# Two freed LSTM state tiles take x of groups 4 to 11, value staging gets a second tile, and scratch writes are queued behind the value moves

## The chip, the cores and the metric

The kernel runs on one core of a Trainium2 chip. The metric is the device time of one execution in microseconds (us); of three runs of the kernel before, the median is 2487.06 us (2484.32 to 2489.86). A profiled execution of its own took 2489.89 us; the span that the profile covers is 2488.1 us of it.

Engines are named as in the profile: PE (TensorE, matmuls), DVE (VectorE), ACT (ScalarE), POOL (GpSimd) and SP (SyncE, which here only issues DMAs). PEld is the loading of a matmul's stationary operand.

## The reference: four layers on x of 128 x 64 x 256

`x` holds 128 batches of 64 nodes with 256 features. Each layer normalizes x over the features, applies relu, and adds the layer's output to x:

```python
h = jnp.maximum(_layernorm(x, axis=-1), 0.0)
x = x + _L0_gnn_ref(h, adj, ...)     # two graph convolutions, then LSTMs over windows of 1 to 4 nodes
h = jnp.maximum(_layernorm(x, axis=-1), 0.0)
x = x + _L1_gnn_ref(h, W, adj)       # attention with 4 heads of 64, masked by adj
...                                  # layer 2: graph convolution and two linears with batch norm
...                                  # layer 3: three graph convolutions
```

The change touches the seam between layer 0 and layer 1. In layer 0, for p = 1 to 4 in turn, an LSTM is run over each window of p nodes, and its last hidden state replaces the features of the window's last node:

```python
for p in range(1, MAX_SKIP + 1):
    nw = Tv // p
    wins = h[:, :nw * p, :].reshape(Bv * nw, p, Hd)
    last = _lstm_last(Wih[p - 1], Whh[p - 1], bih[p - 1], bhh[p - 1], wins)
    idx = jnp.arange(nw) * p + (p - 1)
    h = h.at[:, idx, :].set(last.reshape(Bv, nw, Hd))
```

Layer 1 computes q, k and v from h with one weight matrix, a masked softmax of q k / 8 over the 64 nodes of a batch, and its product with v.

## The kernel before, in words

**Tiling.** The 8192 tokens (batch and node) are 16 groups `g` of 512 tokens, 8 batches each. A group of x is a tile of 128 x 4 x 256 numbers, 512 KB. Layer 0 holds its state with features on partitions, in four tiles `hs[0]` to `hs[3]` (`h0` to `h3`) of 32 batches each, so one of them belongs to four groups of x. They stand in a pool of their own on the right side of the on-chip memory.

**End of layer 0.** The LSTMs with p = 4 run in two passes: `j = 0` works on `h0` and `h1`, `j = 2` on `h2` and `h3`. So `h0` and `h1` are final before the second pass begins. Step t of a pass is done for two units in turn (`i` = 0 and 1) by `next_step`: two gate sets of seven products each (a Strassen-like scheme, `seven`, with its combining sums on ACT, DVE and POOL). During steps t = 1 and 2 of pass `j = 2`, four slots of code turn `h0` and `h1` back to token order: `turn_nodes(j, turned)` transposes 16 nodes by two DVE instructions (L262) into a staging tile and writes it with four DMAs on SP's queue (L265) to a scratch tensor `ys` in HBM. `add_turned(g)` (L271) then adds the scratch to `xs[g]` with an accumulating DMA that POOL issues. At this point only groups 0 to 3 of x are on the chip, and only these are added here.

**Layer 1, the attention loop.** It runs over the 16 groups. Group g does: the first half of the values (`values(hT_all, v, (0,))`: 4 matmuls L873, an ACT copy `vt` L878, 4 DMAs L881 on SP's queue that move the halves of `vt` to the partitions of `v`), the load of x of group g + 5 (L58, SP's queue), the seven products of q and k (L851, combined on ACT, DVE and POOL; the POOL part is L180), the addition of the output of group g - 2 (L959 on DVE, L962 on POOL), the turning of the softmax of group g - 1 (L934, copied by ACT L937), the second half of the values, the accumulating DMA `add_turned(g + 3)` for g = 1 to 12, the transposes of the next group's h (L127, copied by ACT L282, differences on DVE L286, L290, L291), the product of softmax and values of group g - 1 (`attend`, L947), the scores of group g (L898, masked by DVE L905), its softmax (L916, L917, ACT L918), one `turn_nodes(g + 8)` for g < 8 (this turns `h2` and `h3`), and the normalization of group g + 2 (DVE L832 to L837, POOL L836 and L838, ACT L111).

`vt` has one buffer. The tile that `turn_nodes` fills in the loop has one buffer too (tag `hc`). Tiles for x of groups 4 to 15 come from a pool `xres_b` that is opened after the LSTM's pools are closed.

**What sets the order.** Each engine works through its instructions in one order, fixed when the kernel is built; a planner of the tile framework merges the program's pieces by its own estimate of when each can start, with `issue_after(x)` as a lower bound ("not ahead of x"). So a change of buffers or of the program's order can move instructions of other lines as well. Waits are semaphore waits that the framework derives from the tiles.

Of the kernel before, what the change touches and what calls it, by code (L numbers as in the profile page):

```python
# [8 lines left out]
F32 = mybir.dt.float32  # L9
# [5 lines left out]
P = 128  # L15
D = 256
NODES = 64
# [21 lines left out]
def adj_preln_kernel(ctx: ExitStack, tc: tile.TileContext, x_in, adj, vec, bg0, bg1,  # L39
# [17 lines left out]
    def load_x(x, g):  # L57
        nc.sync.dma_start(out=x, in_=x_view[:, g * GT : (g + 1) * GT, :])  # L58
# [181 lines left out]


    with tc.using_default_side("right"):
        hres_pool = tc.tile_pool(name="hres", bufs=1)
        hres = hres_pool.__enter__()
    hs = [
        hres.tile([P, 2, NODES, HB], F32, tag=f"h{i}", name=f"h{i}")
        for i in range(NTOK // (HB * NODES))
    ]

    turned_pool = ctx.enter_context(  # L250
        tc.tile_pool(name="turned", bufs=1, space=bass.MemoryType.DRAM)
# [42 lines left out]
    with tc.tile_pool(name="lw", bufs=5) as lw:  # L294
# [220 lines left out]
        with tc.tile_pool(name="back", bufs=1, reuse_waits="tile") as back_pool, \  # L515
# [196 lines left out]
            for p, nk in ((1, 8), (2, 8), (3, 7), (4, 8)):  # L712
# [7 lines left out]
                for j in range(0, len(units), 2):  # L720
# [23 lines left out]
                    for t in range(1, p):  # L744
                        for i, u in enumerate(two):
                            next_step(t, p, n, u, ws, last_sum if (j, t, i) == (0, 1, 0) else None)

                            if p == 4 and j == 2 and t < p - 1:
                                slot = 2 * t + i - 2
                                if slot == 0:  # L750
                                    room = keep.tile([P, 2, TN, 2, 32], F32, tag="arena", name="turned")
                                for part in range(2 * slot, 2 * slot + 2):
                                    turn_nodes(
                                        part,
                                        room[:, part % 3] if part % 3 < 2 else back_pool.tile(
                                            [P, TN, 2, 32], F32, tag="hc", name="turned"
                                        ),
                                    )
                                if slot > 1:
                                    for x_of_group in range(2 * slot - 4, 2 * slot - 2):  # L760
                                        add_turned(x_of_group)
                            if p == 4 and j == 2 and t == p - 1 and i == 0:

                                h = back_pool.tile([P, GT, D], F32, tag="hc", name="h")
                                ln_relu(xs[0], h)
                                hTs = keep.tile([P, 2, 2, GN], F32, tag="arena", name="hT")
                                hT = features(transposed(h))

    xpool_b = ctx.enter_context(tc.tile_pool(name="xres_b", bufs=1, reuse_waits="tile"))
    for g in range(NK, NG):  # L770
        xs.append(xpool_b.tile([P, GT, D], F32, tag=f"x{g}", name=f"x{g}"))
        if g == NK:
            load_x(xs[g], g)


    def arena(pool):
# [42 lines left out]
        return counted  # L819


    with tc.tile_pool(name="att", bufs=2, reuse_waits="tile") as ap_:
        shifts_made = []

# [40 lines left out]
        def values(hT, v, ks):  # L865


            for k in ks:
                ps = bank((P, 2, D))
                for t in range(2):  # L870
                    tok = (2 * k + t) * P
                    for c in range(2):
# [5 lines left out]
                nc.scalar.copy(vt, ps)  # L878
                for par in range(2):
                    for b in range(2):  # L880
# [92 lines left out]
        last = None  # L973
        for g in range(NG):
            if g == NG - NK + 1:
                hres_pool.__exit__(None, None, None)
                with tc.using_default_side("right"):
                    ar_right = ctx.enter_context(
                        tc.tile_pool(name="arena_r", bufs=NG // 2, reuse_waits="tile")
                    )  # L980
            hT_all, blocks = hT
            v = ap_.tile([P, 2 * GT, P], F32, tag="v", name="v")
            moved = values(hT_all, v, (0,))
            if g + NK + 1 < NG:
                with tc.issue_after(moved):
                    load_x(xs[g + NK + 1], g + NK + 1)
            q, k, finish = queries_keys(blocks)
            if g == 0:
                h = normalized(1)
# [10 lines left out]
            if g == NG - 1:  # L1000
# [590 lines left out]
```

## Time and profile before

| what | value |
|---|---|
| median of 3 runs | 2487.06 us (2484.32 to 2489.86) |
| the profiled execution | 2489.89 us, its span 2488.1 us |
| PE busy | 2455.0 us (99%) |
| DVE, ACT, POOL busy | 1539.1 us (62%), 1126.0 us (45%), 454.7 us (18%) |
| attention loop, first L873 of group 0 to first L873 of group 15 | 1207.88 to 1450.49 us |
| x loads on SP's queue | 27 of 512 KB, median 4.8 us from issue to landing |
| scratch writes on SP's queue | 64 of 128 KB, median 3.5 us |
| accumulating loads of POOL | 16 of 512 KB, median 7.3 us |
| value moves on SP's queue | 128 of 64 KB, median 2.1 us |

Times in the profile are counted from the span's start. A timeline or group line names the engine, the source line and "out<-in" by the program's tile names; what stands in brackets after it is how long the engine had been idle and what released it. Lines of a table over stretches of time give, for each engine, the time that it was busy and in parentheses the number of its instructions. A PE that waits inside a long queue of matmuls can look busy, because the ends of matmuls are modelled.

### The profile page before, as it was taken

How to read it: one execution, taken by the hardware profiler on the slowest of the kernel's cores; microseconds unless marked ns; L12 is line 12 of the kernel's file. 1: busy time of each engine (PE TensorE's matmuls, PEld its weight loads, DVE VectorE, ACT ScalarE, POOL GpSimd, SP SyncE). 2: the span in 40 equal slices, each digit the busy share in tenths (PEclk: the TensorE clock that was granted, in tenths of full speed). 3: DMA queues.
4: the chain of work that ended last, by engine and by line, in shares of the span. 5: the costliest groups of instructions: out<-in, count | busy, mean ns of one | idle time of the engine just before them, and what ended most of it. 6: DMA issues, size and time to landing. Idle time of an engine off the chain costs nothing.

```text
span 2488.1 us, 46519 instructions
## 1 busy us (share of the span) xinstructions
PE 2455.0 (99%) x19628; PEld 2091.2 (84%) x19628; DVE 1539.1 (62%) x2768; ACT 1126.0 (45%) x2026; POOL 454.7 (18%) x392
## 2 busy tenths in 40 slices
PE   9999999999999999999989899999999999999999
PEld 6678888889999988888878764486998898888888
DVE  6668866666566575675687686576556454454544
ACT  4557745444444443443544466564333333333332
POOL 4432211111111111121133331013111111101110
PEclk9999999999999999999999999999999999999999
DMA  3200000000000000160265410010000000000000
GB/s 131 88 2 1 1 17 1 1 1 34 1 1 1 1 1 1 24 92 1 63 117 119 91 40 2 1 48 13 10 9 19 10 10 10 18 10 10 18 10 18
DMA packets 123568, 64.79 MB, mean 26 GB/s; under 512 B 70496, under 2 KB 119776, under 8 KB 123360
## 3 DMA queue, kind: packets, MB, share of 16 engines
q1 hardware_dynamic: 113920, 52.62, 8.2%
q0 software_dynamic: 8448, 8.39, 2.3%
q8 instruction: 154, 2.52, 0.4%
q10 hardware_dynamic: 992, 0.82, 0.1%
q14 instruction: 54, 0.44, 0.1%
HBM read 36.64 MB, written 16.78 MB: 21 GB/s over the span
## 4 chain that ended last, share of the span: by engine, by line
PE 87%; DVE 5%; ACT 2%; DMA 2%; issue 1%; POOL 1%; SPq 1%; DVEq 0%; POOLq 0%; ACTq 0%
PE ps L548 39%; PE ps L1391 16%; PE ps L1436 8%; PE ps L804 4%; PE ps L144 4%; PE ps L1355 3%; PE ps L491 2%; PE ps L851 2%; PE ps L467 2%; PE ps L1173 2%; PE ps L1224 2%; DMA v<-vt 1%; PE ps L873 1%; ACT arena L229 1%; POOL arena L180 1%
## 5 line engine op out<-in xcount | busy, mean ns | idle before, releaser
L548 PE MATMUL ps<-diff,s 128*128 128x256 f32 (+1 forms) x1824 | 393.5, 371 | 0.9 <-DVE diff L668 0.9
L1391 PE MATMUL ps<-arena 128*128 128x256 f32 x1792 | 392.4, 381 | 0.0
L1391 PEld LDWEIGHTS ps<-arena 128*128 128x128 f32 x1792 | 337.9, 190 | 54.0 <-issue 9.3
L548 PEld LDWEIGHTS ps<-diff,s 128*128 128x128 f32 x1824 | 345.9, 190 | 33.8 <-issue 1.6
L562 ACT ACTIVATE gates<-gates,lbias 128x512 f32<-128x512 f32 (+5 forms) x426 | 244.2, 620 | 206.0 <-DVE gates L185 149.3
L180 POOL TENSOR_TENSOR gates<-p 128x512 f32<-128x512 f32 (+1 forms) x115 | 149.2, 1297 | 885.7 <-DVE p L177 834.9
L548 PE MATMUL ps<-h,w 128*128 128x256 f32 (+1 forms) x1028 | 241.0, 371 | 0.0
L548 PE MATMUL ps<-diff,w 128*128 128x256 f32 (+1 forms) x1040 | 238.8, 371 | 1.1 <-DVE p L177 1.1
L548 PEld LDWEIGHTS ps<-diff,w 128*128 128x128 f32 x1040 | 197.3, 190 | 19.7 <-DVE p L177 1.5
L548 PEld LDWEIGHTS ps<-h,w 128*128 128x128 f32 x1028 | 195.0, 190 | 19.2 <-issue 0.5
L562 ACT ACTIVATE gates<-ps,lbias 128x256 f32<-128x256 f32 (+3 forms) x213 | 91.8, 477 | 242.5 <-PE ps L548 242.4
L180 POOL TENSOR_TENSOR arena<-arena 128x256 f32<-128x256 f32 (+1 forms) x73 | 82.0, 1123 | 587.8 <-DVE arena L177 558.1
L229 ACT ACTIVATE arena<-arena 128x512 f32<-128x512 f32 (+1 forms) x160 | 88.7, 582 | 193.4 <-POOL arena L180 101.6
L1436 PE MATMUL ps<-arena 128*128 128x128 f32 x1280 | 149.7, 276 | 0.0
L185 DVE TENSOR_TENSOR gates<-p,ps 128x512 f32<-128x512 f32 (+1 forms) x115 | 76.3, 664 | 113.9 <-PE ps L548 113.7
L1436 PEld LDWEIGHTS ps<-arena 128*128 128x128 f32 x1280 | 145.5, 192 | 1.1
L185 DVE TENSOR_TENSOR arena<-arena,ps 128x256 f32<-128x256 f32 (+1 forms) x73 | 43.5, 597 | 156.7 <-PE ps L1391 87.0
L176 DVE TENSOR_TENSOR p<-p,ps 128x512 f32<-128x512 f32 (+1 forms) x131 | 87.0, 664 | 64.6 <-PE ps L548 46.4
L548 PE MATMUL ps<-state,w 128*128 128x256 f32 (+1 forms) x512 | 116.1, 370 | 0.9 <-ACT p L173 0.8
L189 DVE TENSOR_TENSOR gates<-p,ps 128x512 f32<-128x512 f32 (+1 forms) x115 | 76.6, 666 | 64.2 <-PE ps L548 63.7
L804 PE MATMUL ps<-arena,w 128*128 128x512 f32 x256 | 116.0, 606 | 0.0
L548 PE MATMUL ps<-state,s 128*128 128x256 f32 (+1 forms) x512 | 115.8, 369 | 0.0
(196 smaller groups left out, 4062.6 us busy)
## 6 DMA issues: line engine op xcount, KB each, us to landing
x<-in_x SPq DMA_DIRECT2D x27, 512.0 KB, 4.8
y<-turned SPq DMA_DIRECT2D x64, 128.0 KB, 3.5
x<-y POOLq DMA_DIRECT2D x16, 512.0 KB, 7.3
v<-vt SPq DMA_DIRECT2D x128, 64.0 KB, 2.1
out<-x SPq DMA_DIRECT2D x15, 512.0 KB, 2.9
w<-in_wih SPq DMA_DIRECT2D x4, 1024.0 KB, 7.4
w<-in_whh SPq DMA_DIRECT2D x3, 1024.0 KB, 4.9
arena<-in_l3w SPq DMA_DIRECT2D x3, 1024.0 KB, 5.0
```

The lines of the kernel that those rows point to most:

```text
L144: last = nc.tensor.matmul(pss[b][half * 64 : half * 64 + 64, c, t, :], lhsT=src[rows, t, col : col + 64], rhs=a2[rows, :], start=True, sto ...
L176: nc.vector.tensor_tensor(p1, p1, ps[2], ALU.add)
L180: nc.gpsimd.tensor_tensor(out=out[1][1], in0=p1, in1=p5, op=ALU.add)
L185: nc.vector.tensor_tensor(out[0][1], p1, ps[1], ALU.add)
L189: last = nc.vector.tensor_tensor(to, p, q, ALU.add)
L229: nc.scalar.activation(o, o, func)
L548: nc.tensor.matmul(ps[:, r], lhsT=wc[:, j, :], rhs=bc, start=first and r == 0 and c == 0, stop=True, skip_group_check=True,)
L562: nc.scalar.activation(o, ps, func, bias=lbias[:, col : col + 1])
L804: nc.tensor.matmul(ps, lhsT=w1[:, c, m * P : (m + 1) * P], rhs=a[:, 2 + c, :], start=(c == 0), stop=(c == 1),)
L1355: nc.tensor.matmul(ps[:, t, :], lhsT=w[:, t * P : (t + 1) * P], rhs=b, start=first and t == 0, stop=True, skip_group_check=True,)
L1391: nc.tensor.matmul(ps[:, r, :], lhsT=w[:, c, col : col + P], rhs=b[:, c, :], start=first and r == 0 and c == 0, stop=c == 1, skip_group_ch ...
L1436: nc.tensor.matmul(ps[:, t, :], lhsT=w[:, c, t * P : (t + 1) * P], rhs=b[:, c, :], start=first and t == 0 and c == 0, stop=c == 3, skip_gr ...
```

## The change

The change has four parts.

1. `h0` and `h1` move to a pool of their own, `hx`, which stays open. A new `x_for(i)` takes the memory of `h{i}` for a tile of four groups of x (`four`), appends its quarters to `xs` as groups 4 to 7 (i = 0) and 8 to 11 (i = 1), and issues their four loads. `x_for(0)` is called at the end of slot 2 of pass `j = 2`, `x_for(1)` in step t = 3 for unit 0.
2. In step t = 3, `add_turned` is called for groups 4 and 5 after unit 0 and for 6 and 7 after unit 1. In the attention loop it is called for g = 5 to 12 alone (groups 8 to 15), and x is loaded there only for groups 12 to 15, at g = 4 to 7 (`load_x(xs[g + 2 * NK])`).
3. `vt` gets two buffers. The loop's turned tile gets two buffers in a pool `turn` of its own on the right side, closed with `hres` at g = 13.
4. `turn_nodes` no longer issues its four writes; it returns a function `put_down`. In the LSTM slots it is called at once. In the loop it is called in the next group, after the second half of that group's values.

```diff
+        hx = ctx.enter_context(tc.tile_pool(name="hx", bufs=1, reuse_waits="tile"))
...
-        hres.tile([P, 2, NODES, HB], F32, tag=f"h{i}", name=f"h{i}")
+        (hx if i < 2 else hres).tile([P, 2, NODES, HB], F32, tag=f"h{i}", name=f"h{i}")
...
+    def x_for(i):
+
+        four = hx.tile([P, PER, GT, D], F32, tag=f"h{i}", name=f"x_for_h{i}")
+        for k in range(PER):
+            xs.append(four[:, k])
+            load_x(xs[-1], len(xs) - 1)
...
-        for k in range(4):
-            nc.sync.dma_start(out=to[k], in_=turned[k * 32 : k * 32 + 32])
+
+        def put_down():
+            for k in range(4):
+                nc.sync.dma_start(out=to[k], in_=turned[k * 32 : k * 32 + 32])
+
+        return put_down
...
+                            if p == 4 and j == 2 and t == p - 1:
+                                for x_of_group in range(4 + 2 * i, 6 + 2 * i):
+                                    add_turned(x_of_group)
+                                if i == 0:
+                                    x_for(1)
...
+                                if slot == 2:
+                                    x_for(0)
...
-    for g in range(NK, NG):
+    for g in range(3 * NK, NG):
         xs.append(xpool_b.tile([P, GT, D], F32, tag=f"x{g}", name=f"x{g}"))
-        if g == NK:
-            load_x(xs[g], g)
...
-                vt = ap_.tile([P, 2, D], F32, tag="vt", name="vt", bufs=1)
+                vt = ap_.tile([P, 2, D], F32, tag="vt", name="vt")
...
-            if g + NK + 1 < NG:
+            if 0 <= g - NK < NK:
                 with tc.issue_after(moved):
-                    load_x(xs[g + NK + 1], g + NK + 1)
+                    load_x(xs[g + 2 * NK], g + 2 * NK)
...
-            values(hT_all, v, (1,))
+            moved = values(hT_all, v, (1,))
+            if put_down:
+                with tc.issue_after(moved):
+                    put_down()
+            put_down = None
...
-            if 0 < g <= NG - NK:
+            if NK < g <= NG - NK:
                 with tc.issue_after(shifts_made[g]):
                     add_turned(g + NK - 1)
...
-                    turn_nodes(g + 8, ap_.tile([P, TN, 2, 32], F32, tag="hc", name="turned", bufs=1))
+                    put_down = turn_nodes(
+                        g + 8, tp.tile([P, TN, 2, 32], F32, tag="turned", name="turned")
+                    )
```

No instruction is added or taken away on any engine; what changes is where they stand, which memory they use, and what they wait for.

More of the change, by code (lines that the diff above doesn't have):

```diff
@@ L746, in adj_preln_kernel @@
                             next_step(t, p, n, u, ws, last_sum if (j, t, i) == (0, 1, 0) else None)
+                            if p == 4 and j == 2:
+                                slot = 2 * t + i - 2
+                            if p == 4 and j == 2 and t == p - 1:
[3 more added lines that the diff above has]
+                                    x_for(1)
                             if p == 4 and j == 2 and t < p - 1:
-                                slot = 2 * t + i - 2
                                 if slot == 0:
@@ L757, in adj_preln_kernel @@
                                         ),
-                                    )
+                                    )()
+                                if slot == 2:
+                                    x_for(0)
                                 if slot > 1:
@@ L819, in hidden_out @@
         return counted
+    with tc.using_default_side("right"):
+        turn_pool = tc.tile_pool(name="turn", bufs=2, reuse_waits="tile")
+        tp = turn_pool.__enter__()
     with tc.tile_pool(name="att", bufs=2, reuse_waits="tile") as ap_:
@@ L972, in adj_preln_kernel @@
         wqk_blocks = (*wqk, ss + [wdiff, wsum])
-        last = None
+        last, put_down = None, None
         for g in range(NG):
             if g == NG - NK + 1:
+                turn_pool.__exit__(None, None, None)
                 hres_pool.__exit__(None, None, None)
```

## The prediction

> **What bounds the kernel now.** I read the page first: PE is busy 99% of the span, so time can only come from stretches where PE waits, runs at a lower clock, or merely looks busy. The page's slices put most of the DMA traffic late in layer 0 and in the attention loop, so I cut that loop into its 16 groups, each from its first L873 to the next one's. Columns of this table over stretches: length; busy time of PE, PEld, DVE, ACT, POOL; granted PE clock; DMA share; GB/s.
>
> ```profile
> 1207.88:1219.51 11.63, 11.63 (x118) 10.17 (x116) 7.34 (x10) 7.88 (x15) 1.27 (x1) 1.00 0.34 104
> ...
> 1235.02:1250.26 15.24, 14.17 (x194) 11.80 (x189) 14.33 (x29) 7.44 (x13) 6.32 (x6) 1.00 0.73 118
> 1250.26:1265.45 15.19, 14.50 (x194) 12.09 (x189) 14.23 (x28) 7.96 (x14) 6.33 (x6) 1.00 0.60 113
> 1265.45:1284.70 19.25, 16.24 (x194) 13.77 (x189) 14.08 (x30) 7.97 (x14) 6.33 (x6) 0.90 0.69 129
> ...
> 1299.28:1320.87 21.59, 18.83 (x196) 15.12 (x189) 13.58 (x28) 7.93 (x14) 6.28 (x6) 0.84 0.65 119
> ...
> 1368.03:1390.02 21.99, 18.71 (x222) 15.20 (x221) 12.09 (x26) 8.28 (x15) 6.29 (x6) 0.84 0.56 111
> 1390.02:1409.05 19.03, 15.37 (x194) 13.09 (x188) 12.01 (x25) 8.19 (x15) 6.32 (x6) 0.91 0.44 92
> 1409.05:1422.88 13.83, 13.83 (x196) 12.01 (x189) 11.95 (x26) 7.79 (x14) 6.34 (x6) 1.00 0.43 78
> ...
> 1436.77:1450.49 13.72, 13.69 (x195) 11.91 (x188) 11.71 (x26) 7.71 (x14) 4.92 (x5) 1.00 0.17 41
> sum 242.61, PE 226.63 PEld 190.13 DVE 186.23 ACT 118.66 POOL 84.23; mean PE 15.11 PEld 12.68 DVE 12.42 ACT 7.91 POOL 5.62
> ```
>
> The same matmuls take 13.8 us in groups 12 to 14, when the extra transfers are over, and 15 to 22 us before. The four longest have a clock below 1. Next, the chain of work that ended last, in that stretch (start, length, what):
>
> ```profile
> 1276.91 5.36 DMA v<-vt
> ...
> 1298.04 6.90 DMA v<-vt
> ...
> 1367.33 5.06 DMA v<-vt
> ```
>
> In three of the four long groups the path runs through a value move of 5 to 7 us, against a median of 2.1 us. In the fourth (1390 us) it alternates between such moves and the copy into the single `vt`, which must wait for the move before it. The waits name both:
>
> ```profile
> ACT vt L878 <- DMA v<-vt: 37.6, 9, 6.8
> ```
>
> SP's own order in these groups is: one scratch write, four value moves, three scratch writes, four value moves, one 512 KB load; a scratch write whose transpose is late holds the moves behind it. Last, the place where loads will be added, the LSTM's end (timeline):
>
> ```profile
> 1081.81 5.42 POOL L271 DMA_DIRECT2D x<-y  x4
> 1088.98 0.43 DVE L92 BATCH_NORM_STATS2 st<-x 128x6 f32<-128x256 f32 x1 [2.76 <-DMA x<-y]
> 1096.40 1.78 PE L548 MATMUL ps<-diff,w 128*128 128x256 f32 x7 [1.14 <-DVE p L177]
> ```
>
> DVE stands still until the addition into x of group 0 has landed, and PE loses 1.1 us by it.
>
> [...] PE waits of 2.4 to 3.8 us come with the clock shares of 0.84 to 0.91 above. [...] L286 takes 2.02 us at 1248.11 beside POOL's L180, 0.69 us otherwise.
>
> **The change part by part.** I compared the order of instructions of both programs; counts are equal on every engine.
>
> *Taken out of the loop:* 8 of its 12 loads and 4 of its 12 accumulating loads; together with the second `vt`, and the scratch writes now behind the value moves, this removes all that the three slow moves shared an engine or queue with, but for one load in g = 4 to 7. With two `vt` buffers the copy waits for the move two halves back. On SP a group now costs 8 moves, 4 writes and a load of 0.6 us each, 7.8 us of 13.8, so the queue keeps up; a group's second-half values land about 5 us after their copy, 8 us ahead of their use in the next group's `attend`.
>
> *Moved by the planner:* PE's order becomes that of the undisturbed groups nearly everywhere: 32 matmuls of `attend`, then 32 scores, without q and k products between them. In the groups of 15.8 us at 1336 and 1352 the mixing made PE look busy (15.7) while it waited in pieces.
>
> *Kept:* the DVE transposes (two of 0.69 us, 1.3 us a group, g = 0 to 7) and POOL's accumulating issue (1.33 us, now g = 5 to 12). Their cover is thin. DVE needs 12.0 us in a group without transposes, 13.3 with, of 13.8. The loop from one L286 to the next took 13.78 us in the group at 1235 with the transposes inside, so it ties with PE: I charge 0.3 us, 14.1 us for g = 1 to 4. For g = 5 to 8 POOL's order is pow, product, DMA issue, two L962, then L180, and the scores wait for L180. Groups 2 and 3 before have just that order and a transpose: 15.2 us (15.24, 15.19). I take 15.2 for g = 5 to 7, and 14.2 for g = 8 to 12, where the transposes are gone and POOL's excess is 1.3 us less some slack; bounds 13.8 and 15.2.
>
> The sum for the loop, first L873 of group 0 to that of group 15: 11.6 (g = 0, as before) + 4 x 14.1 + 3 x 15.2 + 5 x 14.2 + 2 x 13.8 = 212.2 us, against 242.6: **30.4 us less**. It holds no half-rate window[...].
>
> *Added to the LSTM's end:* `x_for(0)` stands on SP's queue behind part 5's writes, which end at 1076.8. Its four loads are 2 MB; 1 MB of weights took 4.9 to 7.4 us from issue to landing, so 10 to 15 us, some of it after 1081.8, when POOL issues the additions for groups 0 to 3. DVE stands behind group 0's. Before, it cost 1.1 us; bounds of the increase are 0 (loads done by 1084, when the additions' packets begin) and 7 us of later landing, plus 3.4 us if PE then runs 6.8 us at half rate. I take 1.5, since most of the 2 MB is through by then. Behind the stalled DVE stand the LSTM's sums L176 and L177, which PE waits for. `x_for(1)` comes at 1104 with nothing beside it. The four additions for groups 4 to 7 stand on POOL between two L180; the gaps there are 10 to 11 us long (1131.7 to 1143.1), an issue is 1.3 us, and their writes (last issued at 1103) and loads have long landed. Zero; if that cover were gone, at most 2 x 2.7 us.
>
> *Late next:* the writes move back by a group, but the first addition that needs them (group 8) stays at g = 5; part 11 is issued in g = 4 behind the values' second half, some 6 us ahead of POOL's turn. Zero.
>
> Net: 30.4 - 1.5 = 28.9 us off the profiled span of 2488.1, 2459.2. The execution that holds the span is 2489.9, 2.8 us above the median of the runs; taking the same difference from the median gives 2458.2. I say 2459.
>
> **Rivals.** *(a) DVE and POOL set the pace.* The group stays at 15.5 us (as at 1320.87 to 1336.33) for g = 1 to 12, and only the stalls and half-rate windows go: 11.6 + 12 x 15.5 + 2 x 13.8 = 225.2, 17.4 less, 15.9 net: 2471. For it: DVE at 13.3 of 13.8, POOL's slow order. Against it: the DVE loop of 13.78 us, measured. *(b) Part of the stalls stays*, because the loads of groups 12 to 15 still stand between the halves' moves; half the gain, 2473. Against it: with two `vt` a move has a whole group to land, and group 12 before, with an addition in flight beside its moves, runs in 13.8. *(c) Slower.* The 2 MB of `x_for(0)` delay group 0's addition, and DVE's fixed order passes every microsecond on to PE. Price 1 us per us; it decides once the landing is more than 30 us later, 1119 instead of 1089. The bound above is 7, so only if those loads ran at a quarter of the rate of the weights' would it; say 2492. *(d) Nothing changes*, if the value moves are slow by themselves and not by company: against it, the 2.1 us median.
>
> **How the numbers follow.** Forecast 0.66, (a) 0.15, (b) 0.08, (c) 0.08, with causes that I don't see, (d) 0.03. A measurement of this kernel tells about 0.2%, 5 us, from no change. Faster is forecast, (a) and (b): 0.89; same 0.03; slower 0.08. The forecast's own range is 2447 (all groups at 13.8 and no cost in the LSTM: 37.8 us less, 2449, less 2 of spread) to 2466 (g = 1 to 12 higher by 0.6 us each). With (a) and (b) the range is 2447 to 2475.
>
> **What would show it.** Right: groups of 14 to 15.2 us between first L873s, clock 1.00 through the loop, no wait of the copy into `vt` for a move, value moves near 2.1 us, `attend` unbroken on PE, and DVE's wait for group 0's addition somewhat over 2.8 us. Wrong: groups 1 to 4 at 15 us or more (DVE's loop), a clock below 1 in the loop, scores waiting more than 1.5 us for L180, or a gap of PE over 4 us near 1090.

## The result and the profile after

The changed kernel takes 2457.62 us (median of 4 runs, 2456.48 to 2459.01); the kernel before, run beside it, 2488.3 us. The ratio is 0.9879 (95% interval 0.9862 to 0.9896): 30.7 us faster. The profiled execution took 2458.32 us, its span is 2456.5 us. The prediction said 2459.

The span is 31.6 us shorter (2488.1 - 2456.5). From the start of the first line of the value products in group 0 (L873 before, now L894) to that of group 15, the loop fell from 242.6 to 210.6 us, 32.0 less. It starts 2.5 us later (1210.36 instead of 1207.88), and what stands behind it became another 2.1 us shorter; there the trace before has a half-clock window of PE (a granted clock of 0.50) of 3.4 us at 1485.8 us, and the trace after has none.

The line numbers have moved: L873 is L894, L851 L872, L878 L899, L881 L902, L265 L275, L271 L283, L286 L298, L898 L919, L934 L955, L947 L968, L962 L983, L548 L560. First the table over stretches, one row per group, for the changed kernel (length; busy time of PE, PEld, DVE, ACT, POOL; granted PE clock; DMA share; GB/s):

```profile
1210.36:1221.98 11.62, 11.62 (x118) 10.16 (x116) 7.72 (x11) 8.33 (x16) 1.27 (x1) 1.00 0.12 29
1221.98:1236.97 14.99, 14.12 (x195) 12.04 (x189) 12.01 (x26) 8.98 (x16) 2.46 (x3) 1.00 0.17 42
1236.97:1251.29 14.32, 13.92 (x193) 11.81 (x188) 13.39 (x29) 8.06 (x14) 4.92 (x5) 1.00 0.41 74
1251.29:1265.13 13.84, 13.82 (x195) 11.90 (x189) 12.91 (x28) 7.96 (x14) 4.94 (x5) 1.00 0.43 78
...
1292.80:1307.46 14.66, 14.04 (x195) 11.99 (x189) 13.74 (x27) 7.96 (x14) 6.30 (x7) 1.00 0.86 154
1307.46:1322.55 15.09, 14.14 (x194) 11.93 (x189) 14.14 (x28) 8.06 (x14) 6.25 (x6) 1.00 0.87 163
1322.55:1337.63 15.08, 14.18 (x194) 11.93 (x189) 14.14 (x28) 7.95 (x14) 6.24 (x6) 1.00 0.64 107
...
sum 210.57, PE 205.76 PEld 177.05 DVE 185.22 ACT 120.84 POOL 78.23; mean PE 13.72 PEld 11.80 DVE 12.35 ACT 8.06 POOL 5.22
```

The clock is 1.00 in every group; the long groups of 19 to 22 us are gone. What is left above 14 us are groups 1 and 2, groups 6 to 8 and group 10 (14.39), and in groups 6 to 8 DVE is busy for 13.7 to 14.1 us instead of 12.9.

Second, the view of one tile, `vt`: what its engine waited for ahead of the copy, who waited for the copies and moves of it (L947 is `attend`), and how long its moves took to land. Before:

```profile
  DMA v<-vt: 37.6, 9
...
who waited for it (us, times):
  ACT vt L878: 37.6, 9
  PEld ps L947: 12.2, 10
  PE ps L947: 9.1, 5
...
DMA to landing us min/median/max: 2.0/2.1/6.9
```

After:

```profile
  PE ps L894: 34.1, 10
...
DMA to landing us min/median/max: 2.0/2.3/6.8
```

The copy no longer waits for a move at all, only for its own matmuls, and PE, which before waited for moves five times, 9.1 us in all, doesn't either. But the moves have not become faster: the median has risen from 2.1 to 2.3 us, and the slowest still takes 6.8. This is the first sign that the reason given for the gain needs a test.

Third, the LSTM's end, in the timeline after:

```profile
1081.86 5.42 POOL L283 DMA_DIRECT2D x<-y  x4
1090.52 0.43 DVE L92 BATCH_NORM_STATS2 st<-x 128x6 f32<-128x256 f32 x1 [4.24 <-DMA x<-y]
1097.18 3.07 PE L560 MATMUL ps<-diff,w 128*128 128x256 f32 x7 [1.87 <-DVE p L177]
```

The addition for group 0 is issued when it was before, and lands 1.5 us later; DVE waits 4.24 us instead of 2.76, PE 1.87 instead of 1.14, and a half-clock window of 3.4 us follows (clock 0.50 from 1097.5 us on).

### The profile page after: what moved, and what is told of

Its sections match the earlier page's. It is cut to its first block, busy times and chain, and to the rows that moved or that the text cites. A ratio compares the mean times of both kernels' runs of the same rounds, so it can differ in the third digit from the quotient of the medians.

```text
span 2456.5 us, 46565 instructions
## 1 busy us (share of the span) xinstructions
PE 2435.3 (99%) x19628; PEld 2080.4 (85%) x19628; DVE 1537.5 (63%) x2768; ACT 1128.0 (46%) x2026; POOL 453.8 (18%) x392
## 4 chain that ended last, share of the span: by engine, by line
PE 89%; DVE 6%; ACT 2%; DMA 1%; POOL 1%; issue 1%; SPq 0%; DVEq 0%; POOLq 0%; ACTq 0%
PE ps L560 40%; PE ps L1419 16%; PE ps L1464 8%; PE ps L144 4%; PE ps L822 4%; PE ps L1383 3%; PE ps L872 3%; PE ps L503 2%; PE ps L479 2%; PE ps L1201 2%; PE ps L1252 2%; PE ps L894 1%; ACT arena L229 1%; POOL arena L180 1%; PE ps L955 1%
## 5 line engine op out<-in xcount | busy, mean ns | idle before, releaser
L560 PE MATMUL ps<-diff,s 128*128 128x256 f32 (+1 forms) x1824 | 393.5, 371 | 0.9 <-DVE diff L680 0.9
L560 PEld LDWEIGHTS ps<-diff,s 128*128 128x128 f32 x1824 | 345.9, 190 | 33.8 <-issue 1.6
L180 POOL TENSOR_TENSOR gates<-p 128x512 f32<-128x512 f32 (+1 forms) x115 | 149.0, 1296 | 883.2 <-DVE p L177 832.3
L560 PE MATMUL ps<-diff,w 128*128 128x256 f32 (+1 forms) x1040 | 240.3, 372 | 1.9 <-DVE p L177 1.9
L560 PE MATMUL ps<-h,w 128*128 128x256 f32 (+1 forms) x1028 | 241.2, 372 | 0.0
L560 PEld LDWEIGHTS ps<-diff,w 128*128 128x128 f32 x1040 | 198.1, 191 | 20.7 <-DVE p L177 2.3
L560 PEld LDWEIGHTS ps<-h,w 128*128 128x128 f32 x1028 | 195.3, 190 | 19.4 <-issue 0.5
L180 POOL TENSOR_TENSOR arena<-arena 128x256 f32<-128x256 f32 (+1 forms) x73 | 82.3, 1127 | 587.4 <-DVE arena L177 557.8
L560 PE MATMUL ps<-state,w 128*128 128x256 f32 (+1 forms) x512 | 116.1, 370 | 0.9 <-ACT p L173 0.8
L560 PE MATMUL ps<-state,s 128*128 128x256 f32 (+1 forms) x512 | 115.8, 369 | 0.0
```

Of the source, the lines that this page charges most:

```text
L180: nc.gpsimd.tensor_tensor(out=out[1][1], in0=p1, in1=p5, op=ALU.add)
L560: nc.tensor.matmul(ps[:, r], lhsT=wc[:, j, :], rhs=bc, start=first and r == 0 and c == 0, stop=True, skip_group_check=True,)
```

## The experiments

Two questions: which of the parts made the gain, and what holds groups 6 to 8 at 15 us. The theory of the prediction is that three causes work together: value moves made slow by the loads and additions beside them, the copy that waits for the move because there is one `vt`, and scratch writes that stand ahead of moves on SP's queue. Its rivals are that one of the three is the whole cause. All kernels compute the whole of the reference. Where a run is compared below, "start" is the first value product of group 0, "loop" the time from there to that of group 15, both of the profiled execution.

| kernel | median us | ratio to before (95%) | start | loop |
|---|---|---|---|---|
| before | 2488.3 to 2489.1 in the five sets of runs | 1 | 1207.9 | 242.6 |
| changed | 2457.6 | 0.9879 (0.9862 to 0.9896) | 1210.4 | 210.6 |
| `v_only`: second `vt` alone | 2464.5 | 0.9906 (0.9891 to 0.9921) | 1208.8 | 216.2 |
| `p1`: deferred writes alone | 2488.0 | 0.9996 (0.9987 to 1.0004) | 1208.0 | 241.2 |
| `vp1`: both | 2467.1 | 0.9917 (0.9902 to 0.9932) | 1207.7 | 219.7 |
| `x_only`: x part alone | 2479.1 | 0.9963 (0.9950 to 0.9976) | 1209.5 | 231.8 |
| `after_v1`: changed, one `vt` | 2487.0 | 0.9992 (0.9985 to 0.9999) | 1208.0 | 237.5 |
| `after_p0`: changed, writes at once | 2462.3 | 0.9895 (0.9879 to 0.9912) | 1210.0 | 215.5 |
| `late_x`: changed, first loads a slot later | 2456.4 | 0.9873 (0.9859 to 0.9888) | 1208.0 | 210.7 |
| `k_first`: changed, sum for k first on POOL | 2457.6 | 0.9877 (0.9862 to 0.9892) | 1209.0 | 210.6 |
| `add_last`: changed, addition issued last on POOL | 2453.2 | 0.9856 (0.9842 to 0.9871) | 1210.3 | 206.2 |
| `best`: `late_x` and `add_last` | 2451.7 | 0.9850 (0.9836 to 0.9865) | 1207.7 | 206.2 |
| `v_last`: before, second `vt`, addition last | 2457.2 | 0.9873 (0.9857 to 0.9889) | 1208.0 | 210.9 |
| `p0_last`: `add_last`, writes at once | 2457.8 | 0.9875 (0.9858 to 0.9892) | 1210.2 | 209.7 |

### The second staging tile alone

```diff
-                vt = ap_.tile([P, 2, D], F32, tag="vt", name="vt", bufs=1)
+                vt = ap_.tile([P, 2, D], F32, tag="vt", name="vt")
...
-            mx = ap_.tile([P, NH, 1], F32, tag="mx", name="mx")
+            mx = ap_.tile([P, NH, 1], F32, tag="mx", name="mx", bufs=1)
```

> The kernel before with the second staging tile for values alone (to make room, the softmax maxima have one tile in place of two). Loop before 242.6 us, after 210.6. Theory of three joint causes (slow moves by company, one staging tile, scratch writes ahead of moves): the ACT copy no longer waits for moves, but attend still waits for late values, so a third or so of the 32 us, loop 228 to 236. Theory that the single staging tile is the whole cause: loop 211 to 216, run 2457 to 2462. Theory that the loads and additions alone are the cause: loop within 3 us of 242.6.

Measured: loop 216.2 us, run 2464.5 us. This edit alone takes 26.4 us off the loop; the whole change takes 32.0. The view of `vt` in this kernel (whose lines are those of the kernel before):

```profile
  PE ps L873: 16.6, 5
  DMA v<-vt: 6.1, 1
...
who waited for it (us, times):
  ACT vt L878: 6.1, 1
  PEld ps L947: 0.2, 1
...
DMA to landing us min/median/max: 2.0/3.2/7.1
```

All the loads and additions are still in the loop, and the moves are slower than before, 3.2 us in the median. Still the copy waits once, for 6.1 us, instead of nine times, and `attend` on PE no longer waits for a move. So slow moves need not cost time: they cost it because the copy, and through it `attend`, stood close behind them. The theory of three joint causes expected 228 to 236 us and falls; that of the loads and additions alone expected no change and falls too; that of the single tile comes closest, 216.2 us against its 211 to 216, with a run 2.5 us above what it allowed.

How the tile does it is seen in the order of the two halves. With one `vt`, ACT can't copy the second half of a group before the moves of the first have landed, and in the kernel before the planner has put that copy late in ACT's order: in groups 3 to 9 it starts 14.3 to 22.7 us after its matmuls have ended, while ACT does other work. Its moves are then issued about when the `attend` that reads them begins, and in groups 3 to 8 the last of them lands 5.2 to 7.5 us after that beginning. The chain of the kernel before shows one such place:

```profile
1275.77 0.47 ACT vt L878
...
1276.91 5.36 DMA v<-vt
...
1282.32 1.01 PE ps L947 x13
```

With two, the copy of the second half follows its matmuls by at most 1.9 us, and in the same groups the last move lands 0.2 to 7.2 us before `attend` begins. The half-clock windows, 23.9 us long together in the loop before (6.83, 6.83, 6.83 and 3.41 us, the granted clock 0.50 in each), are gone as well, with 1.00 in every group; half of the 23.9, 12 us, is an estimate of what they cost.

So the second tile works in two ways: waits of the copy disappear, and the planner orders several engines differently (414 of the 19628 places in PE's order hold another instruction). How the 26.4 us divide between the two was not separated. PE's order is not all of it: in group 11 that order is the same in both kernels, and the group falls from 19.03 to 13.66 us; and `attend` mixed with scores, as the planner has it in several groups before, need not cost anything, since group 7 of `v_only` is mixed so and takes 13.53 us.

### The deferred writes alone, and both together

In the kernel before, the diff's part 4, with one turned tile in a pool of its own; `vp1` has the edits of `v_only` as well.

```diff
-            values(hT_all, v, (1,))
+            moved = values(hT_all, v, (1,))
+            if put_down:
+                with tc.issue_after(moved):
+                    put_down()
+            put_down = None
...
-                    turn_nodes(g + 8, ap_.tile([P, TN, 2, 32], F32, tag="hc", name="turned", bufs=1))
+                    put_down = turn_nodes(
+                        g + 8, tp.tile([P, TN, 2, 32], F32, tag="turned", name="turned")
+                    )
```

> The kernel before with the scratch writes of the loop queued behind the next group's second half of values, and nothing else (one turned tile in a pool of its own). Three joint causes: moves no longer stand behind writes whose transpose is late, but still share engines with loads and additions and the copy still waits for the move before: a third or so of the 32 us, loop 228 to 238. Theory that the order of the scratch writes is the whole cause: loop 211 to 216. Theory that the loads and additions alone are the cause: within 3 us of 242.6.

> Both: second staging tile and deferred scratch writes, x loaded and added in the loop as before (one turned tile, one tile for the softmax maxima). Three joint causes: about two thirds of the gain, loop 217 to 226; groups 1 to 4 still carry an addition and so POOL's slow order, 15.1 us rather than 13.8 to 14.3, which alone is about 3 us. Theory that loads and additions alone matter: loop within 5 us of 242.6. Theory that they don't matter: loop 211 to 216, and the LSTM's end stays 2.5 us cheaper, run about 2456 to 2460.

Measured: 241.2 us of loop with the writes alone, no change of the run that can be told (0.9996, 0.9987 to 1.0004). That is what the theory of the loads and additions alone expected, which `v_only` has refuted. With both, 219.7 us, 3.5 more than with the second tile alone. The number of `vp1` lies in what the joint causes expected, but not for their reason: the deferred writes added nothing here. With them the copy waits for moves four times, 19.0 us in all. The longest wait, 8.9 us, is in group 11, for a move of 6.6 us: a copy waits for it even with two tiles, since the two copies before it came back to back. A half-clock window of 3.4 us follows, and that group takes 20.56 us instead of 13.66, 6.9 more, of which the other groups win 3.4 back. The chain of `vp1`, where the copy is L885:

```profile
1364.06 1.09 ACT vt L885 x2
...
1367.33 6.61 DMA v<-vt
...
1374.04 0.06 ACT vt L885
```

### The x part alone, and the change without the second tile

`after_v1` is the changed kernel with this edit; `x_only` has this edit and that of the next section (writes at once), so that parts 1 and 2 of the diff are left.

```diff
-                vt = ap_.tile([P, 2, D], F32, tag="vt", name="vt")
+                vt = ap_.tile([P, 2, D], F32, tag="vt", name="vt", bufs=1)
```

> The x part alone: x of groups 4 to 11 loaded beside the last LSTM steps, four additions there; values keep one staging tile and the scratch writes are issued at once in the loop. Three joint causes: half of the gain or somewhat more, loop 218 to 230, some wait of the staging copy for moves left in groups 4 to 8. Theory that loads and additions alone are the cause: loop 210 to 214, run about 2457. Theory that staging or write order is: loop above 235, run 2482 or more with the 2.5 us that the LSTM's end costs.

> The changed kernel with one staging tile for values again; loads, additions and the deferred writes stay. The second tile alone took 26.4 us of 242.6 off the loop, the x part alone 10.9, the deferred writes alone 1.4. Theory that waits for the one tile are the main cause and the x part only makes them rarer: loop 226 to 232, run 2473 to 2480, copy waiting for moves again. Theory that two of the three are enough whichever they are: loop 211 to 216, run about 2459 to 2463.

Measured: the x part alone takes 10.9 us off the loop and 9.7 off the run; its loop of 231.8 us lies in none of the three ranges, nearest to that of the joint causes (218 to 230). With the deferred writes added but one `vt`, the loop is 237.5 us and the run is 2487.0 us, more than either theory expected (226 to 232 and 211 to 216): all the rest of the change together is worth about 1.4 us of the run without the second tile (the profiled execution, 2482.9 us, is one of its faster ones). So beside a single tile the deferred writes cost 5.7 us of the loop and 8.0 of the run (2479.1 to 2487.0). As in the kernel before, the copy of the second half comes late, in groups 6 to 10 by 14.2 to 20.6 us, and it waits more than ever:

```profile
  DMA v<-vt: 51.9, 13
...
DMA to landing us min/median/max: 2.0/2.1/6.8
```

This run also shows a slow move with no load of x and no scratch write near it. The timeline, POOL and SP's queue:

```profile
1371.83 2.63 POOL L283 DMA_DIRECT2D x<-y  x2
```

```profile
1374.53 24.57 SPq L902 DMA_DIRECT2D v<-vt  x16
```

and the chain in the same stretch:

```profile
1375.88 6.83 DMA v<-vt
1382.71 0.04 issue
1382.76 0.91 PE ps L968 x12
```

SP's queue issues nothing but moves for 24 us, and the move issued at 1375.88 takes 6.83 us. POOL issued two accumulating loads of 512 KB at 1371.8 to 1374.5. In the kernel before, the three slow moves that the prediction showed (issued at 1276.91, 1298.04 and 1367.33 us) also follow an issue of POOL's, by 3.2, 1.2 and 2.4 us. All fourteen traces together agree. Of 1748 moves whose landing the profile tells, 621 were under way at the same time as an accumulating load, and 285 of these took more than 4 us; of the other 1127 only 21 did, all but three of them beside a load of x, and the longest took 5.2 us. So POOL's accumulating loads are the company in which moves are slow; the changed kernel still has eight of them in its loop, and so still has moves of 6.8 us. That is read from times; no run here took these loads out alone.

### The change without the deferred writes

```diff
-                    put_down = turn_nodes(
+                    turn_nodes(
                         g + 8, tp.tile([P, TN, 2, 32], F32, tag="turned", name="turned")
-                    )
+                    )()
```

> The changed kernel with the scratch writes of the loop issued at once, as before; second tile and x part stay. Theory that the deferred writes are worth little: loop 210 to 213, run 2456 to 2460, no wait of the copy for a move. Theory that with the faster groups a late transpose holds the moves on SP's queue: loop above 216, run above 2463, moves' median up and copy or attend waiting for them.

Measured: loop 215.5 us, run 2462.3 us, between the two theories: 4.9 us of loop more than the changed kernel. Groups 5 to 8 take 15.1 to 15.2 us, groups 9 and 10 15.7 and 15.4. In group 5 POOL has the order that groups 6 to 8 have in the changed kernel, so part of this is another matter than writes; it is settled by `p0_last` below. With this run all eight combinations of the three parts are measured. What a part takes off the loop depends on which others are there (us, a minus where it costs):

| part | alone | with the first other part | with the second other part | with both |
|---|---|---|---|---|
| second tile (others: x part, deferred writes) | 26.4 | 16.3 | 21.5 | 26.9 |
| x part (others: second tile, deferred writes) | 10.9 | 0.8 | 3.7 | 9.1 |
| deferred writes (others: second tile, x part) | 1.4 | -3.5 | -5.7 | 4.9 |

The second tile is worth 16 us or more in any company, the x part from 0.8 to 10.9 us, and the deferred writes win clearly only with both others. These are differences of one profiled execution each, and the kernels differ in small buffers besides (the softmax maxima, the turned tile).

### The loads of x for groups 4 to 7 one slot later

```diff
-                                if slot == 2:
-                                    x_for(0)
                                 if slot > 1:
                                     for x_of_group in range(2 * slot - 4, 2 * slot - 2):
                                         add_turned(x_of_group)
+                                if slot == 3:
+                                    x_for(0)
```

> The changed kernel with the loads of x for groups 4 to 7 one slot later, behind the last scratch writes of the LSTM's steps (about 1096 instead of 1077 us). Theory that these loads delay the addition of group 0 and through DVE the end of the LSTM: DVE waits 2.8 us again instead of 4.2, no half-clock window of PE at 1097, first L894 at 1208 instead of 1210.4, run 2.0 to 2.5 us shorter. Rival, the delay moves to later loads or to the additions of groups 2 and 3: start of the loop within 0.5 us of 1210.4.

Measured: DVE waits 3.20 us and not 4.24, the loop starts at 1208.03 us, and its length is unchanged (210.66). The run is 2456.4 us, 1.2 less than the changed kernel's, where the starts of the two profiled executions differ by 2.3. Over the seven kernels here that load x early the start is 1208.0 to 1210.4, 1209.6 in the mean; over the other seven 1207.7 to 1208.8, 1208.0 in the mean. So these loads cost 1.6 us in the mean, and the 2.5 of the first trace is at the upper end. The rest goes with a half-clock window: five of the seven have one of 3.4 us near 1097.5 us, beside a wait of PE of 1.87 to 2.26 us, and start at 1209.5 to 1210.4. The other two (`after_v1`, `k_first`) waited 1.23 and 1.80 us there, have no window, and start at 1208.0 and 1209.0. Of the seven that don't load early none has it.

### What holds groups 6 to 8

The prediction held that the scores wait for POOL's sum for k (L180), which comes last in POOL's order. `k_first` emits that sum ahead of the addition's issue and of both additions of the output:

```diff
...
+            if g > 1:
+                with tc.issue_after(finish.first):
+                    add()
...
-                with tc.issue_after(shifts_made[g]):
+                with tc.issue_after(finish.first):
                     add_turned(g + NK - 1)
```

(`finish.first` is the sum for k; `add` issues the two POOL instructions of `add_output`, which no longer issues them itself. The lines that define both are left out here.)

> The changed kernel with POOL's sum for k (L180) put ahead of POOL's issue of the addition and ahead of the two POOL additions of the output, in all groups. Theory that groups 6 to 8 are slow because scores wait 0.75 us each time for that sum at the end of POOL's order: groups 6 to 8 go from 14.66, 15.09, 15.08 to 13.8 to 14.1, loop 207 to 208, run 3 us shorter. Rival, DVE sets the pace there (14.1 us busy in those groups, transposes and POOL beside it): groups stay at 14.7 or more.

Measured: scores don't wait any more, and nothing is won: loop 210.6 us, run 2457.6 us. In this kernel groups 6 to 9 read

```profile
1291.45:1305.30 13.85, 13.80 (x194) 11.89 (x188) 12.97 (x26) 7.96 (x14) 6.17 (x7) 1.00 0.88 158
1305.30:1320.42 15.12, 13.92 (x194) 11.85 (x188) 14.16 (x28) 8.06 (x14) 6.28 (x7) 1.00 0.74 143
1320.42:1335.52 15.10, 13.95 (x195) 11.83 (x188) 14.16 (x28) 7.94 (x14) 6.25 (x7) 1.00 0.63 107
1335.52:1350.24 14.72, 13.70 (x195) 11.88 (x189) 12.37 (x26) 7.79 (x14) 6.33 (x7) 1.00 0.50 89
```

and PE now waits ahead of the turning of the softmax:

```profile
1311.79 0.98 PE L955 MATMUL ps<-ident,e 128*128 128x128 f32 x7 [1.04 <-ACT e L939]
```

The wait has changed its place; the rival was right that DVE sets the pace. Why DVE is busy for 14.1 us and not 12.9 is seen in one instruction, L298, one of the differences of the next group's h, 128 x 512. Timeline of the changed kernel in group 7, DVE and then POOL:

```profile
1320.50 1.93 DVE L298 TENSOR_TENSOR hT<-hT 128x512 f32<-128x512 f32 x1 [0.81 <-ACT hT L294]
```

```profile
1317.64 3.01 POOL L983 TENSOR_TENSOR x_for_h<-x_for_h,o 128x512 f32<-128x512 f32 x2
1320.11 1.76 POOL L180 TENSOR_TENSOR k<-p 128x512 f32<-128x512 f32 x1
```

L298 takes 1.93 us beside POOL's L180, against 0.69 in groups 3 to 5. In `k_first` it takes 1.94 beside the second addition of the output, the changed kernel's L983. So it doesn't matter which of POOL's operations is last, but that one still runs beside L298. The length goes with the overlap: in groups 10, 11 and 12 of the changed kernel POOL's operations run beside L298 for 0.15, 0.39 and 0.60 us, and it takes 0.71, 0.95 and 1.16 us, each 0.56 us more than the overlap. The price in groups 6 to 8 is 1.24 us (1.93 less 0.69). What makes POOL late, so the new theory says, is the addition's issue of 1.3 us ahead of those operations. `add_last` moves this issue behind them, and nothing else: the order on the other four engines is the same.

```diff
-                nc.gpsimd.tensor_tensor(out=xv[:, :, par, :], in0=xv[:, :, par, :], in1=o, op=ALU.add)
+                summed = nc.gpsimd.tensor_tensor(
+                    out=xv[:, :, par, :], in0=xv[:, :, par, :], in1=o, op=ALU.add
+                )
+            shifts_made.append(summed.ins)
...
-                with tc.issue_after(shifts_made[g]):
+                with tc.issue_after(shifts_made[-1]):
                     add_turned(g + NK - 1)
```

> The changed kernel with one thing moved: in groups 6 to 12 POOL issues the addition after the two additions of the output, not ahead of them (in groups 4 and 5 it is so already). New theory: the issue of 1.3 us pushes POOL's last operation by 1.3 us so that it runs beside DVE's L298, which then takes 1.93 us in place of 0.69; the difference of 1.25 us lengthens DVE's round of 13.84 to 15.09, and the group with it, whichever of POOL's operations is last. Then L298 takes 0.7 us in all groups, groups 6 to 8 take 13.8 to 13.9, the loop 206.8 to 207.5 us, the run about 3.3 us less than the changed kernel's. Rival, the issue itself slows DVE wherever it stands: L298 stays above 1.5 us and the groups at 15.1.

Measured: loop 206.2 us, run 2453.2 us, 4.4 less than the changed kernel (the profile: 4.3 of loop). In group 7, DVE and then POOL:

```profile
1319.16 0.69 DVE L298 TENSOR_TENSOR hT<-hT 128x512 f32<-128x512 f32 x1 [0.82 <-ACT hT L294]
```

```profile
1316.71 2.52 POOL L983 TENSOR_TENSOR x_for_h<-x_for_h,o 128x512 f32<-128x512 f32 x2
1319.19 1.25 POOL L283 DMA_DIRECT2D x_for_h<-y  x1
```

The issue itself now runs beside L298 from 1319.19 on, and L298 keeps its 0.69 us, so the rival falls too: here the issue does not slow this subtraction, and POOL's additions do. In groups 6 to 8 it is 0.69 us each time. The groups:

```profile
1292.69:1306.54 13.85, 13.81 (x194) 11.91 (x189) 12.90 (x28) 7.96 (x14) 6.16 (x7) 1.00 0.83 153
1306.54:1320.40 13.86, 13.81 (x194) 11.90 (x188) 12.90 (x28) 7.96 (x14) 6.18 (x7) 1.00 0.79 153
1320.40:1334.25 13.85, 13.85 (x195) 11.89 (x188) 12.90 (x28) 7.85 (x14) 6.15 (x7) 1.00 0.68 118
```

The gain is a microsecond more than the 3.3 expected, because groups 9 to 14 gave 1.1 as well (82.2 us from group 9 to group 14, against 83.3): there too L298 is back at 0.69 us where it had taken up to 1.16.

### Both moves together

`best` is the changed kernel with the edits of `late_x` and `add_last`.

> The changed kernel with both moves: loads of x for groups 4 to 7 one slot later (took 2.3 us off the start of the loop), and POOL's issue of the addition last in its group. If the two are independent: first L894 at 1208.0, loop 206.8 to 207.5, run about 2452 to 2453. If the loop gives some of it back: 2455 to 2457.

Measured: start 1207.68, loop 206.24 us, run 2451.65 us (2451.28 to 2451.85), 0.9850 of the kernel before. The two gains add up: 1.6 us against `add_last`. This is the fastest kernel here, 6.0 us ahead of the changed one.

### What the x part and the writes are still worth then

`v_last` is the kernel before with the edits of `v_only` and `add_last`; `p0_last` is the changed kernel with those of `add_last` and `after_p0`.

> The kernel before with the second staging tile for values (one tile for the softmax maxima) and POOL's issue of the addition last in its group; x loaded and added in the loop as before, scratch writes at once. If the x part's share beside the second tile is only POOL's order: groups of 15.1 us become 13.8 to 14, loop 206 to 210 where it was 216.2 with the tile alone, run 2454 to 2458, as fast as the changed kernel. If the transfers in the loop cost by themselves: loop 212 to 216, run 2460 to 2465.

> The changed kernel with POOL's issue of the addition last in its group, as before this run with gain, and the scratch writes issued at once. Writes at once cost 4.9 us of loop (215.5 against 210.6) when POOL's order was the old one. If part of that was POOL's order too (group 5 had the slow order there): groups 5 to 8 fall to 13.9, groups 9 and 10, where PE's order mixes attend with the values, stay at 15 to 15.7, loop 209.5 to 210.5 against 206.2 with deferred writes, run 2456 to 2457. If the writes' place on SP's queue costs by itself in groups 5 to 8: loop above 212.

Measured: `v_last` has a loop of 210.9 us and runs in 2457.2 us, as fast as the changed kernel, with x loaded and added in the loop as before; the loop lies 0.9 us above what was expected if the x part beside the second tile were POOL's order alone (206 to 210), and below the rival's 212 to 216. Its groups 2 to 4, 15.2 us each with the second tile alone, take 14.3, 13.9 and 13.9; what is left are groups 8 to 10 at 15.0, 15.2 and 16.2. `p0_last` has 209.7 us: groups 5 to 8 fall to 13.6 to 14.3, so those of `after_p0` were POOL's order, and groups 9 and 10 stay at 15.7 and 15.4. Deferred writes are thus worth 3.4 us (209.7 to 206.2), and they act there, on groups 9 and 10. Three things are mixed in these groups of the two kernels. Where PE's order mixes `attend` with scores alone, a group takes 13.5 us (group 7 of `v_last`) or 13.6 (group 8 of `p0_last`), so this costs nothing. Where it mixes `attend` with the next value products as well and no copy waits, it takes 15.0 to 15.7 us (groups 8 and 9 of `v_last`, group 9 of `p0_last`). Where a copy waits 5.5 us for a move and PE's order is unbroken, 15.4 (group 10 of `p0_last`, 14.3 in `add_last`); with value products mixed in and a wait of 5.9 us, 16.2 (group 10 of `v_last`). So both of the latter seem to cost; no run changed one of them alone.

On top of the second tile and POOL's order the x part is worth 1.3 us of loop (210.9 to 209.7) and costs about 1.6 at the start, so that it wins nothing there: the runs are 2457.2 and 2457.8 us. The second tile with deferred writes and POOL's order, but without the x part, was not run, so what the x part adds to the fastest kernel stays open.

## Why the prediction was right, and where it was not

**The sum.** Forecast 212.2 us of loop, measured 210.6; forecast + 1.5 us at the LSTM's end, measured + 2.5 in this execution and 1.6 over all; forecast 2459, measured 2457.6. That the total agrees so closely is in part luck: the terms below miss by up to 2 us, both ways, and the largest of them came true for another reason than the one given.

**"Taken out of the loop"** is the step that failed, though its sum held. It said that fewer transfers, the second `vt` and the new order of the writes together remove all that the slow moves shared an engine or queue with. Company there was: during the three slow moves of the kernel before, the mean busy share of the 16 DMA engines was 1.03, 0.94 and 0.82, of which POOL's queue had 0.56, 0.51 and 0.61; how the queues divide the engines was not shown. The moves did not become faster (median 2.1 before, 2.3 after, at most 6.9 and 6.8). Eight accumulating loads of POOL remain, and moves are still slow beside them; the second tile hides it: alone it is worth 26.4 us, and all else without it 5.2 of the loop (242.6 to 237.5). Its sentence on the second `vt`, that the copy then waits for the move two halves back, was right, and so was what it expected of the second half's values: their last move lands 5.8 to 9.9 us ahead of `attend`. The expected sign of it, moves near 2.1 us, was met in the median for no good reason. The prediction could have seen this: it had both facts, a move of 5 to 7 us and a copy waiting for the move just before, and a whole group of 13.8 us to hide the first once the second was gone.

**"Moved by the planner"** held: from group 2 on, `attend` and the scores are unbroken on PE. But it was booked as an effect beside the others, and it is in part one of the second tile and of the deferred writes, as the orders of `v_only` and `after_p0` show.

**Groups 1 to 4**, 14.1 us each, 56.4 together: 14.99, 14.33, 13.84, 13.84, together 57.0. DVE's transposes cost at most 0.25 us where nothing disturbs DVE (13.84 against 13.59 in groups 11 and 14, which have none), so the charge of 0.3 us for a tie was not needed in groups 3 and 4. Group 1 is 15.0 to 15.5 in every kernel here, with a wait of PE of 0.5 to 0.9 us at its q and k products.

**Groups 5 to 7**, 15.2 each for POOL's order: the size was nearly right and the place off by one group. Groups 6 to 8 took 14.66, 15.09 and 15.08; group 5 took 13.83, since the addition's issue still stands last on POOL there. So groups 5 to 7 were 43.6 us and not 45.6. The mechanism was named wrongly: not the scores' wait for L180, which is a symptom (`k_first` removed it for nothing), but 1.24 us that DVE's L298 loses beside POOL. The prediction had the same pair before it, 2.02 us beside L180 against 0.69 (in the kernel before, L286 takes 0.69 us in all eleven groups of the loop where no operation of POOL runs beside it), and did not take it for the cause. Rival (a) had this right, that DVE and POOL set the pace, but only for three groups and not for twelve. **Groups 8 to 12**, 14.2 each, 71.0: 15.08, 13.90, 14.38, 13.59, 13.94, together 70.9. Groups 13 and 14, 27.6: 27.5.

**The LSTM's end.** The bound of 0 to 7 us of later landing held: 1.5 us (1089.0 to 1090.5). Mis-sized was what follows from it in this execution, a half-clock window, which the prediction had named among its bounds (6.8 us, the length of three of the windows before, 6.83 us at a clock of 0.50; this one lasted 3.41) and left out of the 1.5 us that it took: the wait of PE beside it was 1.87 us, shorter than the 2.4 to 3.8 that it had read beside such windows. Rival (c) needed 30 us, and was far off. The zeros held: nothing waits for `x_for(1)`, for the four additions or for the later writes.

**Rivals (b) and (d).** That the loop would hold no half-rate window was the author's estimate, and it came true. Clock 1.00 in all groups and no wait of the copy rule out (b), and a ratio of 0.9879 (0.9862 to 0.9896) rules out (d).

## What to carry to other kernels

When a transfer is slow and an engine waits for it, ask first who stands behind it, and give that one a second buffer, before making the transfer faster: here 2 KB per partition were worth 26 us of 2488, and the moves stayed as slow as they were. Then compare the order of the instructions before and after, since the planner may have used the buffer to start something earlier. Where one engine's tensor operations slow another's instruction, as POOL's additions did here with DVE's subtraction (1.93 us against 0.69), put beside it what does not (here the issue of a DMA, with 0.69), and the tensor operations elsewhere. An engine's last operation that others seem to wait for may be a symptom: follow the loop of the engine that has the least slack, and look for an instruction whose duration changes between groups.

## What was unexpected of the hardware

- DVE's subtraction of 128 x 512, L298, takes 0.69 us alone and 1.93 to 1.96 us with POOL additions beside it for 1.5 to 1.6 us, while POOL's issue of a DMA beside it costs nothing (0.69). The POOL operation is slowed as well, 1.28 to 1.76 us for L180.
- Value moves of 64 KB, 2.0 us at best, took 6.8 us with two of POOL's accumulating loads of 512 KB just issued and nothing else on their own queue.
- A wait of PE of 1.87 to 2.26 us at the LSTM's end came with a window of 3.4 us at half clock in five traces; beside waits of 0.88 to 1.80 us there the other nine have none.
- The times of the kernels with one `vt` spread more from execution to execution, by 5.5 us over 4 runs of the kernel before and 10.8 over 20 of `after_v1`, those with two by 0.6 to 5.2 over 4 runs each. That waits for moves which are sometimes slow make the time uncertain would explain it, and was not tested.
